# Moving part of the second block's forward Fourier transforms into the first block of a two-layer kernel

## The chip, the cores and the metric

The kernel runs on one core of one Trainium2 chip. The metric is device time in microseconds for one launch, the median of the runs. The core has five engines that run their own instruction streams in order: TensorE (PE in the profile, its weight loads PEld), VectorE (DVE), ScalarE (ACT), GpSimd (POOL) and SyncE (SP), which in this kernel issues nearly all the DMA transfers.

## The reference, cut to what matters

Two layers run one after the other on an input of 4 batches, 128 channels and 128 x 128 positions, all in float32.

```python
# layer 0, per batch, L = 128*128 positions
xm = relu(xf @ mlp_w1.T + b1) @ mlp_w2.T + b2
x_in, z = split(xm @ in_proj_w.T)                 # 256 channels each
u = silu(causal_conv4(x_in) + conv_b)
dt, Bm, Cm = split(u @ x_proj_w.T, [8, 24])
delta = softplus(dt @ dt_proj_w.T + dt_proj_b)
h[t] = h[t-1] * exp(delta[t] * A) + delta[t] * Bm[t] * u[t]      # 256 channels x 16 states
y = (h[t] . Cm[t]) + u * D
out = (y * silu(z)) @ out_proj_w.T
x1 = silu(group_norm(out, 4 groups)) + x

# layer 1, per batch
a = relu(conv1x1(group_norm(cat(x1, x1), 32 groups)) + agg_b)
weights = softmax(mean(a) @ wg_w.T + wg_b)        # 4 per batch
xf = rfft2(x1)                                    # per image, 128 x 65 complex
product = xf * rfft2(irfft2(xf * filt))           # 4 filters
result = irfft2(sum_f weights[f] * product[f]) + 0.5 * x1
```

The kernel uses that the inner inverse and forward transforms cancel, so that the sum over filters is the square of the spectrum times one weighted filter.

## The kernel before, in words

**First block (`block0`).** A batch is cut into 32 chunks of 512 positions, 128 chunks in all. A chunk is 16 slots long. In each slot VectorE runs two scans (`scans`, L411) over 128 partitions, which hold 32 channels with 4 states each; the decay comes from ScalarE (`exps`, L392), the driving term from GpSimd (`dbu`, L362) or, for every fourth one, from a TensorE transpose (`dbu_turn`, L382). The products with C go to VectorE (L413) or GpSimd (L418), and TensorE adds them over states into `y` (L432). The preparation of the next chunk is spread over the slots of the present one by the table that `pre` returns: each entry is a slot, a phase and a function. For example `z_mm` (L222) stands in slot `NP - 3`, which is slot 13, and its eviction `z_act` in slot 15; `cv_mm` (the folded projection and convolution, L233) in slots 0 and 1, `silu_act` in slot 2.

A dictionary `todo` collects all functions by slot and phase, and a loop at the end of `block0` emits them in the order of the phases: turn, sums, pe, exps, late, act, pool, dbu, early, gate, scans, dve, end. That order is written out by hand (`manual_schedule`) and is the order in which each engine executes. Constants are loaded in `first_constants` before the first chunk and in `later_constants` at the end of slot 4 of the first chunk. Matmul results of the preparation share one PSUM pool `psp` of two rotating buffers (tag `pp`).

**The end of layer 0 (`finish`).** The group norm of a batch needs all of its chunks, so it runs during the chunks of the next batch: in chunks 2 to 17 of that batch two pieces of 512 positions are normalised per chunk, and `x1` is written to DRAM; in the chunks after that `x1` is read again for the aggregation (`agg_mm`, L615, `agg_act`, L619). For the last batch this work is done inside the second block.

**Second block (`block1`).** The work is cut into 64 units: a group of 8 channels (`CC`) of one batch. A unit is three steps of 3, 3 and 2 images. Per step: `over_h` (L788) transforms over h on TensorE, ScalarE evicts half of it (L790), `conjugates` (L795) fills the other half by symmetry on VectorE, `over_w` (L802, L803) transforms over w, ScalarE doubles and squares (L805 to L807), `products` (L813 to L820) multiplies by the weighted filter, GpSimd combines real and imaginary parts (`sums`, L827 and L828), `back_h` and `back_w` (L841, L842, L853) transform back, `residual` (L860) adds the input, and the result is stored. The weighted filter of a unit is made by ScalarE (`term`, L761, four per unit) and GpSimd (`mix`, L767, three per unit). The steps of several units overlap: step t emits `over_h(t)`, `over_w(t - 1)`, `products(t - 2)`, `back_h(t - LAG)` and so on, with `LAG` = 7. The images of a unit (`load`, L754) are loaded one unit ahead, the filters of a channel group (`load_filter`, L748) into one of four buffers.

The order of units: the first 13 channel groups for batches 0, 1 and 2 while batch 3 is being finished, then three groups of batch 3 whose filters were kept, then the last 3 groups for all four batches with the remaining units of batch 3 in between.

Of the kernel before, what the change touches and what calls it, by code (L numbers as in the profile page):

```python
# [26 lines left out]
F32 = mybir.dt.float32  # L27
# [6 lines left out]
P = 128  # L34
# [4 lines left out]
CC = 8  # L39
KEEP = 4  # L40
# [5 lines left out]
def kernel(ctx: ExitStack, tc: tile.TileContext, a: dict, out: bass.AP):  # L46
# [32 lines left out]
    def first_constants(s):  # L79

        s.b1 = col("mlp_b1")
        s.w2 = const("w2", [P, NH, C], a["mlp_w2T"].rearrange("(j p) c -> p j c", p=P))
        s.b2 = col("mlp_b2")
        win = s.win = const("win", [P, 2 * DI], a["in_wT"])
        wck = s.wck = const("wck", [P, KC, DI], a["conv_wT"].partition_broadcast(P))
        s.cb = col("conv_b")
        s.wx = const("wx", [P, NH, NX], a["x_wT"].rearrange("(j p) r -> p j r", p=P))
        s.wdt = const("wdt", [R, DI], a["dt_wT"])
        s.bdt = col("dt_b")
        s.ident = const("ident", [P, P], a["c_ident"])  # L90
        alog = const("alog", [P, NH * NG * ND], a["alog_q"])
# [6 lines left out]
        amat = s.amat = cpool.tile([P, NH * NG * ND], F32, tag="amat", name="amat")  # L98
        nc.scalar.activation(amat, alog, AF.Exp)
        nc.vector.tensor_scalar_mul(amat, amat, -1.0)  # L100
        s.diag = cpool.tile([P, NH, P], F32, tag="diag", name="diag")
        for j in range(NH):
            nc.vector.tensor_scalar_mul(s.diag[:, j, :], s.ident, dvec[:, j : j + 1])

    def later_constants(s):
# [7 lines left out]
        s.wagg = const("wagg", [P, 2, C], a["agg_wT"].rearrange("(j p) o -> p j o", p=P))  # L113
# [8 lines left out]
        s.ihc = const("c_ihc", [H, H], a["c_ihc"])  # L122
        s.ihs = const("c_ihs", [H, H], a["c_ihs"])
        s.iw = const("c_iw", [W, W], a["c_iw"])
        s.sign = const("c_sign", [W, H], a["c_sign"])
# [23 lines left out]
    stats, outs = {}, {}  # L149
# [5 lines left out]
def block0(tc, s):  # L155
# [4 lines left out]
    with ExitStack() as ctx:  # L160
# [7 lines left out]
        dbc = pool("dbc", 2, space=DRAM)  # L168
        psp = pool("psp", 2, space=PSUM)
# [13 lines left out]
        def pre(k):  # L183
# [130 lines left out]
            def rep_load(j):  # L314
# [9 lines left out]
                (NP - 3, "pe", z_mm), (NP - 1, "act", z_act), (NP + 2, "act", z_silu), (3, "pe", xd_mm), (4, "act", xd_act), (5, "pe", dt_mm), (5, "pe", xd_turn),  # L324
# [141 lines left out]

        n_chunks = B * NCH
# [20 lines left out]
        for b in range(B - 1):  # L488
            for at, phase, f in finish(s, io, b, NP + 7, norm, agg):
                todo[at + (b + 1) * NCH * NP, phase].append(f)  # L490
        for n in range(n_chunks * NP):
# [182 lines left out]
def block1(tc, s):  # L674
# [10 lines left out]
    with ExitStack() as ctx:  # L685
        def pool(name, bufs, **kw):
            return ctx.enter_context(tc.tile_pool(name=name, bufs=bufs, **kw))

        p2 = pool("f2", 2)
# [7 lines left out]
        fh, fwr, fwi, ihc, ihs, iw = s.fh, s.fwr, s.fwi, s.ihc, s.ihs, s.iw  # L697
        sign = s.sign.rearrange("w (o r k) -> w o r k", o=1, r=2)
# [23 lines left out]
        units = [(c0, b) for c0 in wait for b in range(B - 1)] + [(c0, B - 1) for c0 in kept]  # L722
        for n, c0 in enumerate(rest):
            units += [(c0, b) for b in range(B)]
# [25 lines left out]
        def load(n):  # L750
            if n < N:
                c0, b = units[n]
                u[n].xt = p2.tile([H, CC, W], F32, tag="xt1", name=f"xt1_{n}", bufs=6)
                nc.sync.dma_start(out=u[n].xt, in_=s.x1[b][c0 : c0 + CC].rearrange("c h w -> h c w"))  # L754

# [29 lines left out]
        def over_h(e, n, m, k):  # L785
            e.pa = psa.tile([W, 3, 2, WF], F32, tag="pa", name=f"pa_{n}_{m}")
# [6 lines left out]
        def conjugates(e, n, m, k):  # L793
            o = e.sa[:, 0:k, :, HH:]
# [3 lines left out]
        def over_w(e, n, m, k):  # L798

            e.px = psx.tile([H, 3, 2, WF], F32, tag="px", name=f"px_{n}_{m}")  # L800
            for q in range(k):
                nc.tensor.matmul(images(e.px)[:, q], e.sa[:, q, 0, :], fwr, start=True, stop=False)  # L802
                nc.tensor.matmul(images(e.px)[:, q], e.sa[:, q, 1, :], fwi, start=False, stop=True)  # L803
            e.xs = p2.tile([H, 2, 3, WF], F32, tag="xs", name=f"xs_{n}_{m}")
# [179 lines left out]
```

## Time and profile before

| | |
|---|---|
| median of 3 runs | 7226.67 us (7223.53 to 7229.71) |
| span of the profiled execution, first to last instruction | 7219.4 us |
| median of the runs less that span | 7.3 us |
| first block, to the first instruction of the second | about 6408 us |
| second block | about 811 us |
| DMA traffic | 1246.27 MB, mean 173 GB/s |

The profile is one execution, taken by the hardware profiler; its own time is known as the span in the table. In its slices each digit is the busy share of an engine in tenths. A row of a group gives the line, the engine, the operation, the tiles written and read, their shape and the count, then the time in which the group was busy and the mean duration of one instruction in nanoseconds, and then the idle time of the engine before these instructions with what ended it. A float32 matmul shows as two records. A row of a timeline gives the start, the duration, the engine and the instruction, with the idle time before it in brackets. "SPq" is SyncE issuing a transfer.

### The profile page before, as it was taken

To read this page: it belongs to the slowest core of one execution; us is meant where nothing else is said; L and a number is where in the kernel's file an instruction comes from. 1 tells how busy PE (TensorE), PEld (TensorE's weight loads), DVE (VectorE), ACT (ScalarE), POOL (GpSimd) and SP (SyncE) were. 2 spreads that over 40 slices of the span, in tenths; PEclk is the share of its full clock that TensorE was granted. 3 is DMA by queue.
4 is the path that set the end of the run, shared out by engine and by line. 5 is a ranking of instruction groups with operands and counts; after the bars stand their busy time and mean duration, and the time that the engine had idled before them with its cause. 6 is when DMAs were issued, how large, how long until landed. Compare 5 with 4: busy or idle time off the path is not lost. (4 is left out here: it accounts for less than half of the span.)

```text
span 7219.4 us, 89408 instructions
## 1 busy us (share of the span) xinstructions
PE 5935.8 (82%) x25908; PEld 2629.2 (36%) x25908; DVE 6925.4 (96%) x8040; ACT 6133.6 (85%) x13583; POOL 6890.8 (95%) x3188
## 2 busy tenths in 40 slices
PE   7888888888878788888788788887787888868999
PEld 2333333322222233332222233332232323348999
DVE  7999999999999999999999999999999999978677
ACT  7888888888888888888888888888888888877876
POOL 7999999999999999999999999999999999977787
PEclk8888888888888898998888899998888898989999
DMA  6766676677777776777777777777787777768666
GB/s 151 160 159 160 151 165 159 151 165 172 180 192 178 182 172 161 175 169 170 190 179 192 174 160 176 171 160 187 179 192 181 169 173 169 161 167 240 183 169 164
DMA packets 864127, 1246.27 MB, mean 173 GB/s; under 512 B 78856, under 2 KB 318608, under 8 KB 863632
## 3 DMA queue, kind: packets, MB, share of 16 engines
q1 hardware_dynamic: 863488, 1240.28, 71.8%
q8 instruction: 204, 3.34, 0.2%
q14 instruction: 291, 2.38, 0.1%
q10 hardware_dynamic: 144, 0.26, 0.0%
HBM read 996.97 MB, written 243.27 MB: 172 GB/s over the span
## 5 line engine op out<-in xcount | busy, mean ns | idle before, releaser
L362 POOL TENSOR_TENSOR hb<-rdu,rB 128x1536 f32<-128x1536 f32 (+2 forms) x1536 | 3608.0, 2366 | 35.1 <-DMA rdu<-dd 32.1
L392 ACT ACTIVATE da<-rdelta,amat 128x512 f32<-128x512 f32 x4096 | 2786.1, 698 | 139.3 <-DVE h L411 134.5
L418 POOL TENSOR_TENSOR hb<-h,rC 128x1024 f32<-128x1024 f32 (+1 forms) x1072 | 2436.8, 2275 | 68.4 <-DVE h L411 53.9
L411 DVE TENSOR_TENSOR_SCAN da<-da,st,hb 128x512 f32<-128x512 f32 x1976 | 2417.4, 1265 | 22.1 <-ACT da L392 15.6
L432 PE MATMUL y<-hb,sel 128*32 128x512 f32 x8192 | 1337.9, 730 | 4.7 <-POOL hb L418 4.1
L382 PE MATMUL b<-ident,bt 128*128 128x128 f32 x4096 | 753.9, 307 | 673.5 <-DVE h L411 539.1
L413 DVE TENSOR_TENSOR hb<-da,rC 128x512 f32<-128x512 f32 x2040 | 1294.3, 672 | 3.0
L411 DVE TENSOR_TENSOR_SCAN h<-da,st,b 128x512 f32<-128x512 f32 x992 | 1256.2, 1266 | 1.5 <-PE b L382 1.5
L411 DVE TENSOR_TENSOR_SCAN h<-da,st,hb 128x512 f32<-128x512 f32 x1000 | 1249.9, 1254 | 1.4 <-ACT da L392 1.0
L233 PE MATMUL pp_cv<-xm,wck 128*128 128x512 f32 x2048 | 1061.0, 665 | 1.4 <-ACT xm L216 0.8
L303 ACT ACTIVATE bt<-pt_dut,xdt 128x256 f32<-128x256 f32 x2048 | 836.3, 470 | 186.0 <-PE pt_dut L292 185.8
L382 PEld LDWEIGHTS b<-ident,bt 128*128 128x128 f32 x4096 | 525.5, 154 | 1242.1 <-DVE h L411 902.5
L414 ACT COPY st<-da 128x1 f32<-128x1 f32 x2040 | 271.3, 159 | 495.0 <-DVE hb L413 494.7
L233 PEld LDWEIGHTS pp_cv<-xm,wck 128*128 128x128 f32 x2048 | 417.3, 215 | 706.5 <-issue 460.8
L767 POOL TENSOR_TENSOR wb<-wb,term 128x1040 f32<-128x1040 f32 x192 | 461.1, 2402 | 89.8 <-ACT term L761 78.6
L292 PE MATMUL pt_dut<-ident,du 128*128 128x128 f32 x1024 | 233.7, 339 | 299.9 <-ACT xdt L285 174.0
L428 PE MATMUL y<-u,diag 128*128 128x512 f32 x512 | 300.9, 671 | 149.7 <-DVE zs L442 147.6
L292 PEld LDWEIGHTS pt_dut<-ident,du 128*128 128x128 f32 x1024 | 132.5, 163 | 618.6 <-POOL du L311 492.3
L392 ACT ACT_TABLE_LOAD x262 | 336.1, 1283 | 11.8 <-DMA rdelta<-dd 7.1
L311 POOL TENSOR_TENSOR du<-delta,u 128x512 f32<-128x512 f32 x256 | 319.6, 1271 | 26.7 <-ACT delta L274 26.7
L432 PEld LDWEIGHTS y<-hb,sel 128*32 128x32 f32 x8192 | 173.3, 116 | 371.4 <-issue 278.0
L266 PE MATMUL pp_dt<-xd,wdt 8*128 8x512 f32 x512 | 281.9, 639 | 31.9 <-ACT pp_o L456 23.4
(145 smaller groups left out, 8082.0 us busy)
## 6 DMA issues: line engine op xcount, KB each, us to landing
rdelta<-dd SPq DMA_DIRECT2D x1024, 256.0 KB, 4.7
rdu<-dd SPq DMA_DIRECT2D x1024, 256.0 KB, 7.8
rC<-bc SPq DMA_DIRECT2D x512, 256.0 KB, 7.5
rB<-bc SPq DMA_DIRECT2D x512, 192.0 KB, 4.7
dd<-delta SPq DMA_DIRECT2D x256, 256.0 KB, 7.4
dd<-du SPq DMA_DIRECT2D x256, 256.0 KB, 5.9
ft<-in_filt_w SPq DMA_DIRECT2D x104, 520.0 KB, 6.9
ob<-o SPq DMA_DIRECT2D x128, 256.0 KB, 2.0
```

What stands on the lines that cost most here:

```text
L233: nc.tensor.matmul(ps["cv", j], w, d["xm"][:, t : t + T], start=t == 0, stop=t == KC - 1)
L292: nc.tensor.transpose(ps["dut"][:, 2 * t + j, :], d["du"][:, j, at : at + P], s.ident)
L303: nc.scalar.activation(d["bt"][:, 2 * h + t, :, q, :], src, AF.Copy, scale=d["xdt"][:, 2 * h + t, R + q : R + q + 1])
L311: nc.gpsimd.tensor_tensor(du, d["delta"][:, j, :], d["u"][:, j, :], ALU.mult)
L362: nc.gpsimd.tensor_tensor(hb[:, p : p + n, :], d["du", j][:, m : m + n, :], d["B"][:, p - 1 : p - 1 + n, :], ALU.mult)
L382: nc.tensor.transpose(b[:, t * P : (t + 1) * P], src, s.ident)
L392: nc.scalar.activation(da, d["delta", j][:, m, :], AF.Exp, scale=s.amat[:, c : c + 1])
L411: nc.vector.tensor_tensor_scan(o, das[q], b, init, ALU.mult, ALU.add)
L413: nc.vector.tensor_tensor(hb[:, p + q, :], das[q], d["C"][:, p + q, :], ALU.mult)
L418: nc.gpsimd.tensor_tensor(hb[:, ps, :], h[:, q, :], d["C"][:, ps, :], ALU.mult)
L432: nc.tensor.matmul(y[m * DG : (m + 1) * DG, :], s.sel, d["hb", j, r][:, p, :], start=False, stop=r == NG - 1)
L767: nc.gpsimd.tensor_tensor(wb, wb, u[n].terms[f], ALU.add)
```

## The change

A new list of functions, `spectrum`, is added to the first block. For batch 0 and for the first nine channel groups of batch 1 it loads images from `x1`, transforms them over h and then over w on TensorE, with both halves of the second transform computed into separate halves of the partitions, and stores the result in a DRAM tensor `spec`. A channel group takes three chunks (3, 3 and 2 images). Batch 0 takes chunks 52 to 99 and batch 1 chunks 100 to 126. The units concerned are 25 of 64.

In the second block such a unit loads its spectrum beside its images, and `over_h`, `conjugates` and the matmuls of `over_w` are left out for it; the doubling and the squares read the loaded spectrum. The order of batches within a group becomes 0, 2, 1 (and 0, 2, 1, 3 in the last groups). The projection `z_mm` moves from slot 13 to slot 14. Four constants that only the second block uses are now loaded there, the aggregation weights share a buffer of the normalisation, and a new constant `fwm` is loaded and negated on VectorE.

```diff
+EARLY = 2
...
-        s.wagg = const("wagg", [P, 2, C], a["agg_wT"].rearrange("(j p) o -> p j o", p=P))
+        s.wagg = s.spare.tile([P, 2, C], F32, tag="xr", name="wagg")
+        nc.sync.dma_start(out=s.wagg, in_=a["agg_wT"].rearrange("(j p) o -> p j o", p=P))
...
-        s.ihc = const("c_ihc", [H, H], a["c_ihc"])
-        s.ihs = const("c_ihs", [H, H], a["c_ihs"])
-        s.iw = const("c_iw", [W, W], a["c_iw"])
-        s.sign = const("c_sign", [W, H], a["c_sign"])
+        s.fwm = const("fwm", [W, 2 * WF], a["c_fwi"])
+        nc.vector.tensor_scalar_mul(s.fwm, s.fwm, -1.0)
...
-    stats, outs = {}, {}
+    stats, outs, spectra = {}, {}, set()
+    spec = [dpool.tile([H, C, 2, WF], F32, tag=f"spec_{b}", name=f"spec_{b}") for b in range(EARLY)]
...
-                (NP - 3, "pe", z_mm), (NP - 1, "act", z_act), (NP + 2, "act", z_silu), (3, "pe", xd_mm), (4, "act", xd_act), (5, "pe", dt_mm), (5, "pe", xd_turn),
+                (NP - 2, "pe", z_mm), (NP - 1, "act", z_act), (NP + 2, "act", z_silu), (3, "pe", xd_mm), (4, "act", xd_act), (5, "pe", dt_mm), (5, "pe", xd_turn),
...
+        def spectrum(b, c0, n):
+
+            g = {}
+
+            def load():
+                g["x"] = p1.tile([s.H, 3, s.W], F32, tag="fx", name=f"fx_{b}_{c0}")
+                nc.sync.dma_start(out=g["x"][:, 0:n], in_=s.x1[b][c0 : c0 + n].rearrange("c h w -> h c w"))
+
+            def over_h():
+                g["pa"] = psp.tile([s.W, 3, 2 * s.WF], F32, tag="pp", name=f"pp_fa_{b}_{c0}")
+                for q in range(n):
+                    nc.tensor.matmul(g["pa"][:, q], g["x"][:, q], s.fh, start=True, stop=True)
+
+            def evict():
+                g["sa"] = p1.tile([s.W, 3, 2 * s.WF], F32, tag="fs", name=f"fs_{b}_{c0}")
+                nc.scalar.copy(g["sa"][:, 0:n], g["pa"][:, 0:n])
+
+            def over_w():
+                half = s.H // 2
+                g["px"] = psp.tile([s.H, 3, 2 * s.WF], F32, tag="pp", name=f"pp_fx_{b}_{c0}")
+                for q in range(n):
+                    re, im = g["sa"][:, q, 0 : s.WF], g["sa"][:, q, s.WF :]
+                    for (data, a, b_), start in (((re, s.fwr, s.fwr), True), ((im, s.fwi, s.fwm), False)):
+                        for at, w in ((0, a), (1, b_)):
+                            o = g["px"][at * half : (at + 1) * half, q]
+                            nc.tensor.matmul(o, data[:, at : at + half], w, start=start, stop=not start)
+
+            def store():
+                x = p1.tile([s.H, 3, 2, s.WF], F32, tag="fq", name=f"fq_{b}_{c0}")
+                nc.scalar.copy(x[:, 0:n].rearrange("h c r k -> h c (r k)"), g["px"][:, 0:n])
+                nc.sync.dma_start(out=s.spec[b][:, c0 : c0 + n], in_=x[:, 0:n])
+
+            return [
+                (4, "pe", load), (12, "pe", over_h), (12, "end", evict), (13, "pe", over_w), (13, "end", store),
+            ]
+
         n_chunks = B * NCH
         todo = defaultdict(list)
         for k in range(n_chunks):
...
+        chunk = NCH + NCH // 2 + 4
+        for b in range(EARLY):
+            for c0 in range(0, C, CC):
+                chunk = max(chunk, (b + 1) * NCH + NCH // 2 + 4)
+                if chunk + 3 > n_chunks:
+                    break
+                for at, n in ((0, 3), (3, 3), (6, 2)):
+                    for slot, phase, f in spectrum(b, c0 + at, n):
+                        todo[slot + chunk * NP, phase].append(f)
+                    chunk += 1
+                s.spectra.add((c0, b))
         for n in range(n_chunks * NP):
             if n % 2 == 0:
                 todo[n - 3, "early"].append(partial(exps, n, (0,)))
...
-        fh, fwr, fwi, ihc, ihs, iw = s.fh, s.fwr, s.fwi, s.ihc, s.ihs, s.iw
-        sign = s.sign.rearrange("w (o r k) -> w o r k", o=1, r=2)
+        def const(name, shape):
+            t = late.tile(shape, F32, tag=name, name=name)
+            nc.sync.dma_start(out=t, in_=s.a[name])
+            return t
+
+        fh, fwr, fwi = s.fh, s.fwr, s.fwi
+        with tc.manual_schedule():
+            sign = const("c_sign", [W, H])
+            ihc, ihs, iw = const("c_ihc", [H, H]), const("c_ihs", [H, H]), const("c_iw", [W, W])
+        sign = sign.rearrange("w (o r k) -> w o r k", o=1, r=2)
...
-        units = [(c0, b) for c0 in wait for b in range(B - 1)] + [(c0, B - 1) for c0 in kept]
+        units = [(c0, b) for c0 in wait for b in (0, 2, 1)] + [(c0, B - 1) for c0 in kept]
-            units += [(c0, b) for b in range(B)]
+            units += [(c0, b) for b in (0, 2, 1, 3)]
...
+                u[n].early = units[n] in s.spectra
+                if u[n].early:
+                    u[n].sx = p2.tile([H, CC, 2, WF], F32, tag="sx", name=f"sx_{n}", bufs=2)
+                    nc.sync.dma_start(out=u[n].sx, in_=s.spec[b][:, c0 : c0 + CC])
...
@@ -783,6 +844,8 @@
 
         @block
         def over_h(e, n, m, k):
+            if u[n].early:
+                return
             e.pa = psa.tile([W, 3, 2, WF], F32, tag="pa", name=f"pa_{n}_{m}")
             for q in range(k):
                 nc.tensor.matmul(images(e.pa)[:, q], u[n].xt[:, m + q, :], fh, start=True, stop=True)
...
@@ -791,6 +854,8 @@
 
         @block
         def conjugates(e, n, m, k):
+            if u[n].early:
+                return
             o = e.sa[:, 0:k, :, HH:]
             nc.vector.tensor_tensor(o, e.pa[:, 0:k, :, 1:], sign.to_broadcast([W, k, 2, HH]), ALU.mult)
 
...
@@ -798,10 +863,16 @@
         def over_w(e, n, m, k):
 
             e.px = psx.tile([H, 3, 2, WF], F32, tag="px", name=f"px_{n}_{m}")
+            e.xs = p2.tile([H, 2, 3, WF], F32, tag="xs", name=f"xs_{n}_{m}")
+            if u[n].early:
+                x = e.x = u[n].sx[:, m : m + k]
+                nc.scalar.activation(e.px[:, 0:k, 0], x[:, :, 1], AF.Copy, scale=2.0)
+                nc.scalar.activation(e.xs[:, 0, 0:k], x[:, :, 0], AF.Square)
+                nc.scalar.activation(e.px[:, 0:k, 1], x[:, :, 1], AF.Square)
+                return
             for q in range(k):
                 nc.tensor.matmul(images(e.px)[:, q], e.sa[:, q, 0, :], fwr, start=True, stop=False)
                 nc.tensor.matmul(images(e.px)[:, q], e.sa[:, q, 1, :], fwi, start=False, stop=True)
-            e.xs = p2.tile([H, 2, 3, WF], F32, tag="xs", name=f"xs_{n}_{m}")
             nc.scalar.activation(e.xs[:, 1, 0:k], e.px[:, 0:k, 1], AF.Copy, scale=2.0)
             nc.scalar.activation(e.xs[:, 0, 0:k], e.px[:, 0:k, 0], AF.Square)
             nc.scalar.activation(e.px[:, 0:k, 1], e.px[:, 0:k, 1], AF.Square)
...
-            nc.vector.tensor_tensor(sq[:, 1, 0:k], e.px[:, 0:k, 0], e.xs[:, 1, 0:k], ALU.mult)
+            twice = e.x[:, :, 0] if u[n].early else e.xs[:, 1, 0:k]
+            nc.vector.tensor_tensor(sq[:, 1, 0:k], e.px[:, 0:k, 0], twice, ALU.mult)
```

More of the change, by code (lines that the diff above doesn't have):

```diff
@@ L90, in first_constants @@
         s.ident = const("ident", [P, P], a["c_ident"])
-        alog = const("alog", [P, NH * NG * ND], a["alog_q"])
+        amat = s.amat = const("amat", [P, NH * NG * ND], a["alog_q"])
         dvec = col("D")
@@ L96, in first_constants @@
             nc.vector.tensor_mul(wck[:, t, :], win[:, 0:DI], wck[:, t, :])
-        amat = s.amat = cpool.tile([P, NH * NG * ND], F32, tag="amat", name="amat")
-        nc.scalar.activation(amat, alog, AF.Exp)
+        nc.scalar.activation(amat, amat, AF.Exp)
         nc.vector.tensor_scalar_mul(amat, amat, -1.0)
@@ L168, in block0 @@
         dbc = pool("dbc", 2, space=DRAM)
+        s.spare = p2
         psp = pool("psp", 2, space=PSUM)
@@ L687, in pool @@
             return ctx.enter_context(tc.tile_pool(name=name, bufs=bufs, **kw))
+        late = pool("late", 1)
         p2 = pool("f2", 2)
```

## The prediction

> **What bounds the kernel now.** I read the page first: span and engine totals, then the slices.
>
> ```profile
> span 7219.4 us, 89408 instructions
> PE 5935.8 (82%) x25908; PEld 2629.2 (36%) x25908; DVE 6925.4 (96%) x8040; ACT 6133.6 (85%) x13583; POOL 6890.8 (95%) x3188
> DVE  7999999999999999999999999999999999978677
> POOL 7999999999999999999999999999999999977787
> ```
>
> VectorE and GpSimd are full for 35 of 40 slices, the first block; in the last five, the second block, they are not. So I asked for the busy times by stage. The first two rows are one chunk each (one under the normalisation of the batch before, one under its aggregation), the others are stages of the second block, cut where a unit's last residual ends.
>
> ```profile
> core 0: us, PE busy (x) PEld busy (x) DVE busy (x) ACT busy (x) POOL busy (x), PEclk, DMA share, GB/s
> 3512.60:3562.90 50.30, 39.96 (x154) 14.71 (x153) 50.27 (x54) 43.27 (x95) 50.06 (x24) 0.87 0.76 184
> 4509.50:4558.10 48.60, 41.31 (x160) 15.55 (x159) 48.41 (x51) 42.87 (x97) 47.72 (x22) 0.93 0.73 167
> 6462.00:6658.60 196.60, 170.38 (x1438) 165.44 (x1438) 169.41 (x376) 152.88 (x302) 145.60 (x76) 0.98 0.84 253
> 6658.60:6716.00 57.40, 54.26 (x469) 52.73 (x468) 45.95 (x109) 46.04 (x98) 47.26 (x25) 1.00 0.63 170
> 6716.00:6795.40 79.40, 79.40 (x612) 70.94 (x611) 53.53 (x127) 65.12 (x145) 58.32 (x31) 1.00 0.73 205
> 6795.40:6848.60 53.20, 53.20 (x409) 47.45 (x408) 35.67 (x84) 43.38 (x97) 38.84 (x21) 1.00 0.62 174
> 6848.60:6937.80 89.20, 88.67 (x781) 87.52 (x780) 70.46 (x172) 73.74 (x155) 77.62 (x41) 1.00 0.44 119
> ```
>
> A first-block chunk is VectorE's: 0.03 us idle of 50.30 in the first row, while TensorE and ScalarE have 10 and 7 us free. In the second block TensorE binds from 6716 on (no idle at all to 6848.6), and before that, under the last batch's normalisation, nothing is full on average but the DMA engines are 84% busy.
>
> **The part that shrinks: the second block.** Of 64 units, 25 lose both forward transforms (16 of batch 0, 9 of batch 1). The costs come from the groups of the stage 6716 to 6795:
>
> ```profile
> L767 POOL TENSOR_TENSOR wb<-wb,term 128x1040 f32<-128x1040 f32 x18 | 43.2, 2402 | 11.8 <-ACT term L761 11.0
> L788 PE MATMUL pa<-c_fh,xt 128*128 128x130 f32 x96 | 13.6, 275 | 0.0
> L795 DVE TENSOR_TENSOR sa<-pa,c_sign 128x384 f32<-128x384 f32 (+1 forms) x18 | 9.2, 513 | 24.2 <-ACT sa L790 24.2
> ```
>
> A unit sends TensorE 48 matmuls (8 pa, 16 px, 16 pz, 8 po). In the steady units near 6940 it takes 10.72 us with TensorE never idle, so the 24 forward ones are half: 5.36 us. VectorE loses three conjugate multiplies, 3 x 0.513 = 1.5 us; ScalarE three copies, 3 x 0.43 = 1.3 us (row L790, 432 ns). The three squares and doublings stay, now reading SBUF. GpSimd keeps everything: 3 x 2.402 + 1.30 + 1.29 (sums, L827 and L828) = 9.8 us. So an early unit can fall to about 10 us and no lower, GpSimd being next; an ordinary one stays at 10.72, or 13.29 with three aggregation matmuls in it. The unit order puts an ordinary unit between two early ones in the first nine groups, and one early to two ordinary ones in groups 9 to 12.
>
> By stages: 6716 to 6795.4 is six units of 13.29, four of them early: 4 x 10.1 + 2 x 12.9 = 66, -13 us. 6795.4 to 6848.6, two of four early: 2 x (13.29 - 10.1), plus a little carried into the next, -7. 6848.6 to 6937.8, two of eight: -3.5 (10.9 becomes 9.9, and 0.8 carried each). 6658.6 to 6716, three of five: -5. After 6937.8 only three units are early, and each stands directly before one that waits for its images: TensorE sat 4.2 us at 6988 until "xt<-x" landed, queued behind four filter loads. That wait swallows what the early unit gains; with its spectrum load also in the queue I take +1.
>
> Normalisation, 6462 to 6658.6, fifteen units. They run at 12.67 us with three stalls, none of it from one full engine: the waits name ScalarE, VectorE and TensorE in turn. Without the forward half an early unit should run near 10.8, so two of three give 11.4, and with the stalls about 178, -18 us. **A DMA rule against this.** Three such units (6474.7 to 6512.9) keep the DMA engines 88% busy at 264 GB/s, which at 100% is 300 GB/s: 10.0 MB per three units. Two spectra add 2 x 0.53 MB, so at 300 GB/s the floor is 11.1 / 0.300 = 37 us, 12.3 us a unit and a gain of only 12 us. The Trainium skill, "DMA: Bandwidth & Descriptors", section Specifications, gives some 358 GB/s from HBM to a core: 11.1 / 0.358 = 31 us, 10.3 a unit, no floor at all and -18. These packets are mostly 512 bytes, so I lean to the row; 4 KB runs of a spectrum should be cheaper than that mean, so -16.
>
> **A clock rule against it.** An early unit leaves TensorE idle 4 us. The skill, "TensorE: Matmul & The Clock Gate", part 1, says that an idle window of about 3.4 us halves the clock. This trace agrees (unit at 6981 to 6999: granted clock 0.81 after the 4.2 us gap; one unit takes 17.98 us). But the idle comes in three parts of 1.3 us between back transforms; by the row the clock stays at 1.0 and the sum stands. By the rule, had it come in one piece, each ordinary unit behind an early one would pay up to 1.7 us, half a window, 16 x 1.7 = 27 us, and the gain would be gone.
>
> **What is added, block two's start.** Four constants (sign, ihc, ihs, iw) are now issued by SyncE ahead of the first images. SyncE stood from 6406.4 to 6408.3 waiting for the last "ob<-o" to land; four issues at 0.43 us fit there: nothing, and 1.7 us if they don't. The first spectrum, 0.53 MB at 300 GB/s, goes ahead of the filters for which GpSimd starts: +1.6.
>
> **What is added, the first chunk.** The new tile fwm is negated on VectorE in the list where before only two memsets stood:
>
> ```profile
> 66.85 0.06 DVE L127 MEMSET eps<- 128x1 f32 x1
> 66.89 0.17 DVE L129 MEMSET ones<- 128x128 f32 x1
> 75.88 0.43 SPq L71 DMA_DIRECT2D c_ihc<-in_c_ihc  x1
> ```
>
> VectorE runs in order and reaches the place at 66.85. The load of fwm is the sixteenth constant, in the place of c_ihc, issued at 75.88; c_fwi, the same array, took 2.3 us to land. So VectorE stands still from 66.9 to about 78.3, and behind it wait the scans, then GpSimd's products with C, ScalarE's exponentials (their buffers come free by scans), all of the chunk. 11.4 us, of which 1 to 2 us come back, since the chunk after has that much VectorE idle: +11 (with the multiply). If GpSimd's later DMA wait (4 us idle near 101) absorbs part, +5.
>
> **What is added, 75 chunks.** Chunks 52 to 126 each take a third of a group: one load (0.2 MB) and one store (0.2 MB) on SyncE's queue, six forward and twenty-four half-wide matmul instructions, two ScalarE copies of 128x390. VectorE and GpSimd get nothing. DMA: +0.4 MB on 8.3 to 9.3 MB, 5%, with the engines at 73 to 76%: hidden. SyncE: the store waits for its copy late in slot 13; next in its queue are normalisation loads for five slots later and the second replica load at slot 16. Hidden. ScalarE: 2 x 0.48 = 0.96 of 6 to 7 us free. TensorE: a 130-column instruction goes every 0.11 us (612 in 79.4 us is 0.13 with long ones among them); 6 x 0.12 = 0.7, and 24 x 0.12 = 2.9, or 1.5 if the two halves run side by side as the four quarter-wide y<-hb matmuls do (8 in 1.06 us, against 4 full ones of pp_z in 1.99). 2.2 to 3.6 us, twice that at half clock, into 7 to 11 free. So averages hide it all; the question is the place. Slots 12 to 14:
>
> ```profile
> 3002.18 1.99 PE L222 MATMUL pp_z<-xm,win 128*128 128x512 f32 x4
> 3007.25 0.62 PE L382 MATMUL b<-ident,bt 128*128 128x128 f32 x3 [3.08 <-DVE h L411]
> ...
> 4552.74 1.30 ACT L392 ACTIVATE da<-rdelta,amat 128x512 f32<-128x512 f32 x2
> 4554.60 2.44 DVE L411 TENSOR_TENSOR_SCAN da<-da,st,hb 128x512 f32<-128x512 f32 x2
> ```
>
> TensorE has a hole of 3.08 us there in which the half transform fits, and moving pp_z one slot later costs nothing in it. The exponential that the scan at 4554.60 needs ends about 4553.4: 1.2 us of room. The two copies stand ahead of it and take 0.96, and the second waits for TensorE's half transform, up to some 0.5 us more. So in tight chunks VectorE may lose 0 to 0.4 us; chunk at 3007 has 1.5 us of room and some ScalarE idle, and loses nothing. About half the chunks tight: 75 x 0.5 x 0.2 = +8, bounds 0 and 75 x 0.6 = 45 (at half clock). Not below nothing by more than 5: the filled hole may keep the clock up.
>
> **Sum.** +11 + 8 + 1.6 - 16 - 5 - 13 - 7 - 3.5 + 1 = -23. The profiled span 7219.4 becomes 7196.5; the median of the runs, 7226.67, is 7.3 above that span, so 7203.8.
>
> **Rivals.**
> - Larger gain. The DMA engines give more than 300 GB/s and elasticity between units lets TensorE's spare time reach the ordinary units (-24, -6, -18, -9, -8, -3), first-chunk wait +5, chunks 0, start +1.6: -61, 7165. For it: unit at 6500, 4.13 MB in 12.85 us, 321 GB/s. Against: small buffers (one pa, two px).
> - Nothing measurable. The normalisation stage is held by DMA entirely (0 in place of -16): -7, 7220.
> - Slower: the copies wait on TensorE in nearly every chunk. Priced at 0.75 us of VectorE time per chunk, 75 chunks cost 56 in place of 8: 7252. For it: 0.03 us of VectorE idle means that nothing can be made up; ScalarE's queue is in order. It decides from 0.41 us a chunk (31 / 75). Against: 1.2 to 1.5 us of room before 0.96 us of copies.
>
> **Numbers.** A measurement of this kernel tells some 0.2%, 14.5 us, from no change. Forecast 0.50 (own range 7186 to 7222), larger gain 0.18, nothing 0.18, slower 0.14. Within the forecast's range a sixteenth or so lies inside 0.2%. Faster 0.48 + 0.18 = 0.66, within 0.2% 0.20, slower 0.14. Range 7172 to 7246.
>
> **What would show it.** Right: an early unit near 10 us with GpSimd fullest, ordinary ones unchanged; VectorE idle for some 11 us at 67 in the first chunk; chunk lengths 48.4 to 50.3 as before within 0.3 us; "pp_z" after the new matmuls without a wait that reaches VectorE. Wrong: chunks longer by over half a microsecond, normalisation units still 12.7, TensorE at half clock after early units, or more "xt<-x" waits.

## The result

The changed kernel takes 7174.42 us (median of 4 runs, 7164.74 to 7175.93) against 7225.45 us for the kernel before (4 runs, 7223.53 to 7229.71): a ratio of 0.9926, 95% interval 0.9914 to 0.9939. That is 51 us; the forecast was 23, and 7174 lies nearer to the "larger gain" rival's 7165 than to the forecast's 7203.8. The profiled executions differ by 7219.4 - 7173.6 = 45.8 us, and this is the sum that the terms below must meet. The other 5 us lie in which executions were profiled: the median of the runs is 7.3 us above the profiled span before, and 0.9 us after. Run again beside the last experiments, the changed kernel gave 7173.34 us, ratio 0.9925 (0.9911 to 0.9940), and a span of 7171.8 us.

The page of the kernel after, its first two parts:

```profile
span 7173.6 us, 91384 instructions
PE 5904.2 (82%) x26708; PEld 2626.8 (37%) x26708; DVE 6892.9 (96%) x7966; ACT 6143.9 (86%) x13658; POOL 6892.5 (96%) x3188
DVE  6999999999999999999999999999999999989777
POOL 6999999999999999999999999999999999988887
```

Only the first slice of the first block and the last five slices differ. Busy time by stage, after; the columns are those of the prediction's table, and each row stands for the row at the same place there (chunks 70 and 90, then the second block cut after the same units). "Unit 9" below is the stretch from the end of unit 8's last residual to the end of unit 9's; since steps overlap, the forward transforms that run in it are mostly those of unit 12:

```profile
core 0: us, PE busy (x) PEld busy (x) DVE busy (x) ACT busy (x) POOL busy (x), PEclk, DMA share, GB/s
3522.03:3572.32 50.29, 40.72 (x183) 16.10 (x182) 50.26 (x54) 43.94 (x97) 50.10 (x24) 0.90 0.78 193
4519.86:4568.76 48.90, 41.61 (x176) 15.52 (x175) 48.48 (x51) 43.24 (x99) 48.10 (x23) 0.93 0.71 171
6466.80:6639.10 172.30, 126.01 (x960) 118.28 (x960) 156.18 (x346) 139.52 (x271) 146.90 (x76) 0.95 1.02 317
6639.10:6690.40 51.30, 43.38 (x332) 41.34 (x333) 42.02 (x101) 42.67 (x89) 46.66 (x24) 0.93 0.80 224
6690.40:6756.60 66.20, 62.11 (x445) 52.49 (x444) 48.91 (x117) 60.33 (x135) 58.26 (x31) 1.00 0.94 270
6756.60:6803.20 46.60, 45.62 (x337) 39.24 (x336) 33.08 (x80) 41.30 (x93) 39.06 (x21) 1.00 0.77 226
6803.20:6889.20 86.00, 82.59 (x708) 81.17 (x707) 68.87 (x169) 71.62 (x150) 77.30 (x41) 0.98 0.49 136
6889.20:7169.50 280.30, 251.68 (x2119) 248.46 (x2117) 203.94 (x484) 194.47 (x398) 217.85 (x114) 0.96 0.69 182
```

A chunk with a third of a spectrum in it is as long as before (50.29 against 50.30; 48.90 against 48.60). Over the 75 chunks the mean length differs by 0.01 us, single chunks by up to 1.9 us either way. In the stage under the normalisation, the first row of the second block, TensorE lost 44 us of work and the stage 24 us, with the DMA engines at 1.02 of their time (the profile adds up the times of packets, which can overlap). (The start of a stage is the end of its predecessor's last residual.)

The terms of the prediction's sum, each read from the two traces at the same chunk or unit:

| term | predicted, us | measured, us |
|---|---|---|
| first chunk, fwm | +11 | +10.7 (offset at chunk 52) |
| 75 chunks with a spectrum | +8 | -1.4 (chunk 52 to the block's last eviction) |
| start of the second block | +1.6 | -4.5 (to the end of unit 0) |
| normalisation, 15 units | -16 | -24.3 |
| next four stages | -5, -13, -7, -3.5 | -6.1, -13.2, -6.6, -3.2 |
| tail | +1 | +2.7 |
| sum | -23 | -45.9 |

The second execution of the changed kernel gives +11.3, -1.5, -4.6, -24.8 for the first four.

### The profile page after: what moved, and what is told of

Same layout as the page of the kernel before. It is cut to its first block, busy times and chain, and to the rows that moved or that the text cites. A ratio compares the mean times of both kernels' runs of the same rounds, so it can differ in the third digit from the quotient of the medians.

```text
span 7173.6 us, 91384 instructions
## 1 busy us (share of the span) xinstructions
PE 5904.2 (82%) x26708; PEld 2626.8 (37%) x26708; DVE 6892.9 (96%) x7966; ACT 6143.9 (86%) x13658; POOL 6892.5 (96%) x3188
## 3 DMA queue, kind: packets, MB, share of 16 engines
q8 instruction: 210, 3.44, 0.2%
## 4 chain that ended last, share of the span: by engine, by line
DVE 41%; ACT 29%; issue 11%; PE 10%; DMA 5%; POOL 3%; SPq 1%; DVEq 0%; ACTq 0%; POOLq 0%
DVE da L412 20%; DVE h L412 12%; ACT da L393 12%; DVE hb L414 5%; ACT L393 3%; DMA rdelta<-dd 2%; ACT L275 2%; ACT delta L275 2%; ACT bt L304 2%; POOL hb L363 2%; DVE zs L443 1%; PE y L433 1%; POOL hb L419 1%; ACT L242 1%; DMA xt<-x 1%
## 5 line engine op out<-in xcount | busy, mean ns | idle before, releaser
L433 PE MATMUL y<-hb,sel 128*32 128x512 f32 x8192 | 1313.4, 717 | 2.9 <-POOL hb L419 2.7
L234 PE MATMUL pp_cv<-xm,wck 128*128 128x512 f32 x2048 | 1014.3, 640 | 1.6 <-ACT xm L217 0.8
L234 PEld LDWEIGHTS pp_cv<-xm,wck 128*128 128x128 f32 x2048 | 395.9, 204 | 651.0 <-issue 422.1
L312 POOL TENSOR_TENSOR du<-delta,u 128x512 f32<-128x512 f32 x256 | 318.8, 1267 | 25.8 <-ACT delta L275 25.8
L223 PE MATMUL pp_z<-xm,win 128*128 128x512 f32 x512 | 274.5, 634 | 51.8 <-ACT fq L497 46.2
```

The source lines that it names most:

```text
L234: nc.tensor.matmul(ps["cv", j], w, d["xm"][:, t : t + T], start=t == 0, stop=t == KC - 1)
L312: nc.gpsimd.tensor_tensor(du, d["delta"][:, j, :], d["u"][:, j, :], ALU.mult)
L433: nc.tensor.matmul(y[m * DG : (m + 1) * DG, :], s.sel, d["hb", j, r][:, p, :], start=False, stop=r == NG - 1)
```

## The experiments

Ratios are to the kernel before, run on the same chip beside each. Times of stages come from each kernel's one profiled execution.

### The wait for fwm, and what it uncovered

The wait itself is where it was expected; VectorE's timeline of the kernel after in chunk 0 (start, duration, instruction, idle time before):

```profile
65.16 1.22 DVE L412 TENSOR_TENSOR_SCAN h<-da,hb 128x512 f32<-128x512 f32 x1 [0.25 <-ACT da L393]
77.38 0.23 DVE L124 TENSOR_SCALAR fwm<-fwm 128x130 f32<-128x130 f32 x1 [11.00 <-DMA fwm<-in_c_fwi]
```

First the negation alone was moved:

```diff
-        nc.vector.tensor_scalar_mul(s.fwm, s.fwm, -1.0)      # later_constants, chunk 0
+        todo[3 * NP + 4, "end"].append(lambda: s.nc.vector.tensor_scalar_mul(s.fwm, s.fwm, -1.0))
```

> The changed kernel with the negation of fwm moved from chunk 0 to chunk 3, so that VectorE never stands for the load. My theory: the wait in chunk 0 is carried undiminished to the end of the first block, so chunk 1 starts 9 to 11 us sooner than in the changed kernel (about 106 us in place of 116.6) and the whole takes 7163 to 7166 us against 7174. Rival: later chunks or the normalisation stage have room that swallowed the wait, and the whole stays within 7171 to 7177 us.

Measured: 7169.87 us, ratio 0.9929 (0.9914 to 0.9944), between the ranges of both theories and not told from the changed kernel's 0.9926. Chunk 1 starts at 110.6 us, 5.9 sooner than in the changed kernel's trace, and chunk 4 is 0.6 us later again. Neither theory had the reason. The 11 us wait is gone, but two multiplications on VectorE got longer. Its timeline in this kernel, with weff0's product (weff in the rows) in chunk 0 and the negation in chunk 3:

```profile
78.08 10.37 DVE L132 TENSOR_SCALAR weff<-wagg,gn_gamma 128x128 f32<-128x128 f32 x1
...
223.00 6.54 DVE L511 TENSOR_SCALAR fwm<-fwm 128x130 f32<-128x130 f32 x1
229.46 2.46 DVE L411 TENSOR_TENSOR_SCAN da<-da,st,hb 128x512 f32<-128x512 f32 x2
```

and GpSimd's at the second place:

```profile
220.15 3.61 POOL L362 TENSOR_TENSOR hb<-rdu,rB 128x1024 f32<-128x1024 f32 x2
223.69 2.39 POOL L418 TENSOR_TENSOR hb<-h,rC 128x1024 f32<-128x1024 f32 x1
226.01 3.44 POOL L362 TENSOR_TENSOR hb<-rdu,rB 128x1536 f32<-128x1536 f32 x1
235.53 2.35 POOL L418 TENSOR_TENSOR hb<-h,rC 128x1024 f32<-128x1024 f32 x1 [6.08 <-DVE h L411]
```

A negation that takes 0.23 us while GpSimd stands took 6.54 us, and ends at 229.54, just after GpSimd's last instruction in a row (226.01 + 3.44 = 229.45). Scans and tensor_tensor instructions beside the same GpSimd work keep their usual times (every tensor_tensor of L413 in the kernel before takes 0.66 to 0.69 us). They differ from the multiplications that wait in more than the operation: in this kernel one of their two inputs lies in PSUM. So both parts went to ScalarE:

```diff
-        nc.vector.tensor_scalar_mul(s.fwm, s.fwm, -1.0)
+        todo[3 * NP + 4, "end"].append(lambda: s.nc.scalar.mul(s.fwm, s.fwm, -1.0))
...
-        nc.vector.tensor_scalar_mul(weff0, s.wagg[:, 0, :], s.gam[:, 0:1])
-        nc.vector.scalar_tensor_tensor(weff0, s.wagg[:, 1, :], s.gam[:, 1:2], weff0, ALU.mult, ALU.add)
+        nc.scalar.activation(weff0, s.wagg[:, 0, :], AF.Identity, scale=s.gam[:, 0:1])
+        nc.scalar.activation(pb0[:, P : 2 * P], s.wagg[:, 1, :], AF.Identity, scale=s.gam[:, 1:2])
...
+        nc.vector.tensor_add(weff0, weff0, pb0[:, P : 2 * P])
```

> The changed kernel with the negation of fwm done by ScalarE in chunk 3, and the two products of weff0 in chunk 0 done by ScalarE too, with one tensor_add left to VectorE. In the run that moved the negation on VectorE it took 6.54 us in place of 0.23, and weff0's first product 10.37 us in place of 2.79: both stood until GpSimd had no instruction running. My theory now: VectorE's tensor_scalar waits for GpSimd, so this version, which has none left there, starts chunk 1 at 99 to 101 us (104.1 before, 116.6 changed), and the whole is 13 to 17 us shorter than the changed kernel, 7157 to 7162 us. Rival: the 11 us of chunk 0 are a wait for something else that comes back in another place; chunk 1 starts later than 106 us and the whole stays above 7167 us.

Measured: 7156.66 us, ratio 0.9905 (0.9890 to 0.9920). Chunk 1 starts at 103.1 us, 13.4 sooner than in the changed kernel; 4.2 us of new waiting, for ScalarE, kept it from the 99 to 101 expected. From chunk 52 on the first block stays 13.7 to 17 us ahead of the changed kernel. So a wait of VectorE in chunk 0 is carried to the end of the block in full.

### Are the spectra free in the first block, and is the gain theirs?

```diff
-                u[n].early = units[n] in s.spectra
+                u[n].early = False
```

> The changed kernel whose first block makes and stores all spectra, while the second block ignores them and does every forward transform itself. My theory: the first block ends about 9 us later than before, as in the changed kernel (all of it from the wait in chunk 0), and the second block takes what it took before or 1 to 3 us more (constants loaded at its start), so 7233 to 7240 us against 7225 before. Rival: part of the 55 us that the second block gained comes from the other order of batches and from the constants, and not from the spectra; then the second block is shorter than before here too, and the whole is 7205 to 7228 us.

Measured: 7235.07 us, ratio 1.0018 (1.0009 to 1.0027): the whole is as my theory had it, the parts not quite. The first block ends 8.3 us later than before, and from chunk 52 on loses nothing (it is 10.1 us behind there). The second block takes 8.8 us more than before, not 1 to 3: its start 2.6, and the normalisation stage 6.1:

```profile
6473.00:6675.70 202.70, 173.43 (x1438) 168.99 (x1439) 169.97 (x375) 152.92 (x302) 145.53 (x76) 0.97 0.81 245
```

To see whether the order of batches makes those 6 us, the kernel before got that order alone:

```diff
-        units = [(c0, b) for c0 in wait for b in range(B - 1)] + ...
+        units = [(c0, b) for c0 in wait for b in (0, 2, 1)] + ...
-            units += [(c0, b) for b in range(B)]
+            units += [(c0, b) for b in (0, 2, 1, 3)]
```

> The kernel before with one edit: the batches of a group come in the order 0, 2, 1. In the run that ignored the spectra the normalisation stage took 202.7 us in place of 196.6 before. My theory: the order alone costs these 6 us, so this stage takes 201 to 204 us and the whole 5 to 8 us more than before. Rival: the 6 us come from the constants loaded at the second block's start and the changed places in memory; then the order makes no difference beyond 2 us.

Measured: 7222.66 us, ratio 0.9998 (0.9989 to 1.0007); the stage takes 196.4 us (6466.8 to 6663.2). The order does nothing, and the theory falls. Looked at unit by unit, the two kernels differ in how many units are long and at a lower clock. Units 8 and 9 of the kernel before; unit 9 is one of those whose images are loaded behind the filters of the next group:

```profile
6551.40:6564.10 12.70, 11.29 (x99) 10.91 (x98) 11.27 (x26) 10.25 (x22) 9.73 (x6) 1.00 0.99 259
6564.10:6579.40 15.30, 12.77 (x102) 12.61 (x102) 11.47 (x26) 10.11 (x21) 9.66 (x6) 0.89 0.81 270
```

Such a filter-loading unit takes 12.7 to 13.7 us at clock 1.00, or 15.1 to 15.8 at 0.89. Before, two of the five are long (units 9 and 12), and the same two with the other order; with spectra ignored, four (3, 9, 12 and 15); units 3 and 15 are 2.2 and 2.8 us longer than before, 5.0 of the 6.1. In each long unit TensorE waits once for 2.5 to 3.0 us, in all but one of these eight for images; in the others, no wait is longer than 2.3 us. TensorE's waits for images in the whole stage, before and with the spectra ignored:

```profile
PE pa L788 <- DMA xt<-x: 8.2, 4, 2.7
PE pa L851 <- DMA xt<-x: 13.7, 5, 3.0
```

These 5.5 us more are nearly the 6.1. That the waits make the long units is shown by a run that comes up again under "The tail": the kernel before with images loaded ahead of filters. In it no wait for images is left in the stage, all fifteen units take 12.7 us at clock 1.00, and the stage is 6.5 us shorter than before:

```profile
6467.90:6658.00 190.10, 168.28 (x1435) 162.52 (x1435) 168.66 (x375) 153.21 (x302) 145.73 (x76) 1.00 0.86 261
```

Why the images come later with the spectra ignored than before stays open. In the changed kernel the filter-loading units are early ones; they show a clock of 0.84 or 0.85 too, but TensorE is busy for only 7.4 to 7.8 of some 11 us in them, and they are shorter than their neighbours.

What a spectrum chunk has left was measured by adding ScalarE work to it:

```diff
-                nc.scalar.copy(x[:, 0:n]..., g["px"][:, 0:n])
+                for _ in range(3):
+                    nc.scalar.copy(x[:, 0:n]..., g["px"][:, 0:n])
```

> The changed kernel with the copy of each spectrum (pp_fx to fq) done three times in a row, 0.98 us more of ScalarE's time in each of the 75 chunks. My theory: a spectrum chunk is free because its ScalarE work fits into the time that is left before the exps of slot 15 are due (0.5 to 1.7 us in the changed kernel's chunks); 0.98 us more does not fit in the tight chunks, and the stretch from chunk 52 to the end of the first block gets 5 to 40 us longer. Rival: ScalarE's queue has room enough elsewhere, and the stretch stays within 3 us.

Measured: 7202.75 us, ratio 0.9969 (0.9957 to 0.9980), as expected. The stretch from chunk 52 to the end of the block is 34.4 us longer than before, 35.9 longer than in the changed kernel: 0.48 us a chunk for 0.91 us of copies (0.98 in a chunk of three images, less in one of two). VectorE's waits in the stretch (us in total, times, longest), in the kernel after:

```profile
engine line waited for: us in total, times, longest us
DVE da L412 <- ACT da L393: 11.4, 6, 2.9
```

with the copies tripled:

```profile
DVE da L412 <- ACT da L393: 32.3, 35, 3.9
```

and before, without spectra:

```profile
DVE da L411 <- ACT da L392: 13.9, 15, 2.0
```

So a chunk has room for the one copy and some 0.4 us more, on average, and then the room is gone. The spectra themselves fitted.

### What limits the normalisation stage?

Two runs changed only the transfers of early units. One loads the first unit's spectra alone (of 25 loads it leaves out 24, not the 34 of its expectation):

```diff
-                if u[n].early:
+                if u[n].early and n:
+                    u[n].sx = u[0].sx
+                elif u[n].early:
```

> The changed kernel, which loads the spectra of the first unit only and uses them for all early units (so it leaves out 34 loads of 0.53 MB and its result is not the reference's). My theory: the normalisation stage is now set by the DMA engines at 317 GB/s; without 9 or 10 loads of 0.53 MB it shrinks by up to 16 us, until VectorE's 156 us of work is next, so the stage takes 157 to 163 us in place of 172.3 and the whole 7159 to 7166 us. Rival: the stage is set by the order of the engines' work and not by transfers, and stays at 170 to 173 us, the whole at 7171 to 7176 us.

```profile
6468.50:6634.90 166.40, 124.72 (x960) 116.73 (x960) 155.39 (x346) 140.04 (x271) 146.27 (x76) 0.96 0.98 297
```

The other copies each spectrum once more, from DRAM to DRAM:

```diff
                     nc.sync.dma_start(out=u[n].sx, in_=s.spec[b][:, c0 : c0 + CC])
+                    nc.sync.dma_start(out=s.spare_spec[:, c0 : c0 + CC], in_=s.spec[b][:, c0 : c0 + CC])
```

> The changed kernel with one more transfer in each early unit: the spectra that it loads are also copied within the chip's memory, 0.53 MB read and 0.53 MB written, with no engine's work added. My theory: the DMA engines are full in the normalisation stage, so each of its early units gets 1.5 to 3 us longer: the stage 187 to 203 us in place of 172.3, the whole 7189 to 7210 us, and later stages, where DMA has room, hardly move. Rival: no change beyond 3 us.

```profile
6465.65:6647.30 181.65, 131.83 (x960) 124.90 (x960) 156.35 (x346) 139.65 (x271) 146.25 (x76) 0.91 1.03 329
```

Measured: 7162.96 us, ratio 0.9920 (0.9905 to 0.9935), and 7189.52 us, ratio 0.9956 (0.9939 to 0.9973). Without the loads the stage is 5.9 us shorter, with the copies 9.4 us longer. Both directions are as my theory had them and both sizes in the stage are too small: it asked for 9 to 15 less and at least 15 more. The whole times lie in its ranges, since the stages behind shrank and grew by some 4 us too. Transfers matter here, but below their price: taking 5.2 MB away (317 GB/s x 172.3 us less 297 x 166.4) returned 5.9 us, where they take 16 us at 317 GB/s. The rate is no constant: by the rows' shares the spectra took 12.7 us of the DMA engines' time (1.02 x 172.3 less 0.98 x 166.4), some 410 GB/s, and the rest of the traffic moves at 303 (297 / 0.98). And VectorE's 155 us of work are 93% of the 166.4. Neither is a bound by itself.

Then the spectra of batch 1 were left out:

```diff
-EARLY = 2
+EARLY = 1
```

> The changed kernel with spectra of batch 0 alone; the nine units of batch 1 in groups 0 to 8 do their forward transforms themselves again. My theory: 27 chunks with a spectrum less change nothing in the first block (within 2 us); in the second, where both kinds of unit count, about half of the gain behind the start goes: the stage from unit 0 to unit 15 takes 180 to 188 us (172.3 with both, 196.6 with none), the stretch from unit 15 to unit 30 takes 172 to 182 us (164.2 with both, 190.0 with none), and the whole is 7191 to 7203 us. Rival: in the normalisation stage the transfers alone set the time, so that the five units of batch 1 there are worth nothing; then it stays at 172 to 176 us.

```profile
6466.40:6644.60 178.20, 145.11 (x1200) 138.29 (x1200) 162.07 (x362) 147.10 (x287) 145.44 (x76) 0.99 0.96 294
```

Measured: 7184.35 us, ratio 0.9941 (0.9926 to 0.9956), under the range of my theory; the stage lies between the two theories' ranges. Of the stage's 24.3 us, batch 0's units bring 18.4 and batch 1's 5.9; of the 25.8 us between the ends of units 15 and 30, 20.6 and 5.2. With five units of each batch in the first and five and four in the second, an early unit of batch 0 is worth about three times one of batch 1 that is added to it. The row of units shows why in part: between two ordinary ones, an early unit also shortens its neighbour (11.2 us in place of 12.7), since steps of several units overlap; and the early unit of batch 0 is the one that loads filters, where the long units were. All units of this run but one have clock 1.00 in this stage.

### The tail

In the kernel after TensorE waits 23.6 us in the tail for images. The view of waits there, after:

```profile
PE pa L851 <- DMA xt<-x: 23.6, 6, 5.3
```

```diff
+                    load(n + 1)
                     for ft in loads[n]:
                         load_filter(ft)
-                    load(n + 1)
```

> The changed kernel with one edit in the second block: at the start of a unit the next unit's images are loaded ahead of the filters, not behind them. My theory: units 40, 43, 47, 50, 54 and 57, which take 12.7 to 18.8 us in place of 10.7, stand only because their images queue behind eight filter loads; they fall to about 10.8 us each and the whole is 20 to 27 us shorter than the changed kernel. Rival: the filters are needed as early as the images, so the wait moves from the images to them and the whole stays within 5 us.

Measured: 7139.65 us, ratio 0.9882 (0.9868 to 0.9897). Against the changed kernel's 0.9926 that is 32 us, more than expected; by the traces the tail is 33.4 us shorter. The wait for images is gone, and so are the lower clocks that came behind it:

```profile
6885.50:7132.40 246.90, 240.83 (x2119) 238.03 (x2117) 201.19 (x484) 192.91 (x398) 218.04 (x114) 1.00 0.77 207
```

The same edit on the kernel before:

> The kernel before, with the one edit that images are loaded ahead of filters in the second block. With it on the changed kernel, the tail from unit 38 to unit 63 fell from 280.2 to 246.9 us; before, this tail takes 277.6 us. My theory: the waits for images in the tail are as large before as after, so it falls to 246 to 252 us here too and the whole is 26 to 34 us shorter than before, 7190 to 7198 us; the three early units of the tail are then worth at most 3 us. Rival: the changed order of batches makes these waits, the kernel before has few of them, and the edit gives it less than 15 us.

```profile
6936.50:7191.30 254.80, 253.27 (x2262) 252.69 (x2261) 206.50 (x492) 197.74 (x407) 218.19 (x114) 1.00 0.74 197
```

Measured: 7198.72 us, ratio 0.9960 (0.9945 to 0.9975), just above the expected range, and a tail of 254.8 us in place of 277.6, 22.8 less where 26 to 32 was expected. The rival is refuted, but my bound on the early units was wrong: in tails without waits they are worth 254.8 - 246.9 = 7.9 us, three units at 2.6 each. In the changed kernel that gain was turned into longer waits for images (13.9 us before, 23.6 after), and the tail got 2.7 us longer. With the images first in both kernels, the change is worth 0.9960 - 0.9882 = 0.0078 of the time, some 56 us, so its gain does not hang on these waits. In the normalisation stage the edit does nothing for the changed kernel (172.3 us without it):

```profile
6467.10:6639.15 172.05, 126.29 (x960) 118.62 (x960) 156.09 (x346) 139.64 (x271) 146.41 (x76) 0.95 1.01 316
```

### All together

```diff
-                chunk = max(chunk, (b + 1) * NCH + NCH // 2 + 4)
-                if chunk + 3 > n_chunks:
+                chunk = max(chunk, NCH + NCH // 2 + 4 if b == 0 else 2 * NCH + NCH // 2 + 4)
+                if chunk + 3 > n_chunks or c0 >= 13 * CC:
```

with the ScalarE edit and the order of loads above:

> Three edits together on the changed kernel: VectorE's negation of fwm and products of weff0 go to ScalarE (7156.7 us alone, ratio 0.9905), images are loaded ahead of filters in the second block (7139.7 us alone, 0.9882), and the spectra are made for the first 13 groups alone, batch 0 in chunks 52 to 90 and batch 1 from chunk 91 for 12 groups, none for the last three groups. If the gains add up: 0.9926 less 0.0021 less 0.0044 is 0.9861, 7125 us, and three more early units of batch 1 in groups 9 to 11, in place of the three of batch 0 in the last groups, give 0 to 6 us more: 7118 to 7126 us. Rival: the parts share one slack and do not add up, above 7133 us.

> The changed kernel once more, unedited, for a comparison on the same chip as these three: 7168 to 7176 us. Theories do not differ on it.

Measured: 7129.08 us, ratio 0.9865 (0.9848 to 0.9881), 44 us under the changed kernel's 7173.34 on the same chip, and the shortest time here. It lies above my theory's range and under the rival's: the two edits alone would add up to 0.9861, 7125 us, so they nearly do, and the choice of groups adds nothing. By the traces it gains, against the changed kernel, 5.0 us from unit 19 to unit 30 and 2.2 from there to unit 38, and its tail has the 254.8 us of a tail without early units, 7.9 more than with them.

## Why the prediction was wrong

The direction and the mechanism in the second block were right, the size was not: half of the gain was missing from the sum.

- **The first chunk, +11:** right, measured +10.7. The idle 11.0 us lies where the prediction put it. That GpSimd's later idle time would absorb part did not happen: it stood too, behind the scans. That the sum meets to 0.3 us is luck: weff0's first product takes from 1.14 to 10.37 us in the three traces with the chunk 0 of the kernel before, and against the one with the other order of batches the offset at chunk 52 is only 6.9 us.
- **75 chunks, +8:** mis-sized; measured -1.4, and -1.8 with the spectra made but not used; the other traces with these 75 chunks unedited lie between -1.1 and -4.7, so they cost nothing. The step that failed is "about half the chunks tight: 75 x 0.5 x 0.2". The room was real (1.2 us) and so were the copies (0.96 us), but 0.96 fits into 1.2. The half microsecond more, in which ScalarE's second copy waits for TensorE's half transform, did not come: in none of the 75 chunks did ScalarE stand idle before that copy. In the timeline of chunk 70 after, the 24 half-wide matmuls take from 3564.27 to 3565.81, 1.5 us, the lower of the two prices given, and pp_z follows them with 0.27 us of waiting (0.6 us a chunk over all 75), which does not lengthen the chunk:

```profile
3564.27 0.44 PE L493 MATMUL pp_fx<-c_fwr,fs 128*64 128x130 f32 x4 [0.17 <-ACT fs L483]
...
3565.54 0.27 PE L493 MATMUL pp_fx<-fwm,fs 128*64 128x130 f32 x1
3565.75 1.13 PE L223 MATMUL pp_z<-xm,win 128*128 128x512 f32 x2
3567.15 1.13 PE L223 MATMUL pp_z<-xm,win 128*128 128x512 f32 x2 [0.27 <-ACT fq L497]
```

  The tripled copies show where the rival "slower" would begin: 0.91 us more in each chunk, on average, costs 36 us.
- **Start of the second block, +1.6:** the sign was wrong. It counted the constants and the first spectrum; with the spectra ignored, the start costs 2.6 us. Left out was the saving: the forward transforms of units 0 to 3 run before the end of unit 0, and three of these four units (0, 2 and 3) are early. That is worth the difference, 2.6 + 4.5 = 7.1 us.
- **Normalisation, -16:** mis-sized; measured -24.3. Two steps failed. The first is the floor of 300 GB/s, which made -16 of -18: the engines gave 317 GB/s over the stage. The page "DMA: Bandwidth & Descriptors" of the Trainium skill, section Specifications, states some 358 GB/s; the estimate from it, -18 without a floor, was nearer than the row's -12, and units 9 and 10 of the changed kernel come near that rate (355 and 349 GB/s between 6558.7 and 6581.5), and unit 7 passes it (369 GB/s from 6535.0 to 6547.0). The second is that the sum kept the stage's stalls. It read that the waits name ScalarE, VectorE and TensorE in turn; TensorE's 8.2 us of waits for images were not counted. Without them the kernel before takes 190.1 us (images ahead of filters), and the changed kernel with the same edit 172.1, so the work saved is 18.0 us, the prediction's own figure. The rest, some 6.5 us, are the stalls: in the changed kernel the units behind the filter loads are early, do no forward transform, and TensorE does not wait for images in them. The sign "ordinary ones unchanged" failed as well: the ordinary units of this stage take 11.4 to 12.0 us in place of 12.7.
- **The clock rule:** the clock was wrong, the time right. The granted clock did fall, to 0.83 to 0.85, in seven of the first nineteen units (3, 6, 9, 12, 15, 16 and 18), where the prediction had it stay at 1.0. TensorE's longest wait in the normalisation stage is 2.3 us, so here the clock fell without the idle window that the prediction's rule asks for. Six of the seven are early units, in which TensorE has room, and none of the six is longer than its neighbours. The 27 us that were weighed did not come.
- **The four stages after it:** -29.1 for -28.5. Here one engine, TensorE, was the bound before, and counting its instructions was enough.
- **Tail, +1:** measured +2.7, by the mechanism named.
- **Span to median, +7.3:** the last step added the 7.3 us by which the median stood above the span before; after, it is 0.9.

Of the 23 us of span that the sum missed, then, 9.4 are the chunks, 6.1 the start, 8.3 the normalisation stage; the rest nearly cancels. The "larger gain" rival had this stage (-24) and the chunks (0) right, and most of the stages behind it and the first chunk too favourable.

## What to carry to other kernels

Before an instruction is put into a full engine's list, look at what it waits for: here one 0.23 us negation made VectorE stand for 11 us, while work on the emptier engines in 75 chunks cost nothing until the gap before the next due exponential was used up. Where one engine is full, count its instructions; where none is, a byte rate read from another mix is not a floor, and a stall that is kept in the sum needs its cause. In a queue that is served in order, what is needed first goes first: one line moved was worth 32 us where the whole change gave 51.

## What the hardware showed that was not expected

**VectorE's tensor_scalar can wait for GpSimd through several of its instructions.** weff0's first product, 128x128 float32, took 1.14, 2.79, 6.84, 10.37 and 10.37 us in five kernels (before, after, before with loads swapped, e_fwm, before with the other order), with the same operands. In e_fwm it lasted through the rest of the GpSimd instruction that was running and four more, until GpSimd had no work; in the kernel after, it got through at GpSimd's first change of instruction. The Trainium skill, "SBUF — State Buffer", section "Summary: rules for kernel authors", says that the second to issue is blocked until the first one finishes, and in section "Who interferes with whom" it counts tensor_scalar among the instructions that can take the ports that VectorE and GpSimd share. The waits agree; that one can last over several instructions of the other engine is what these runs add. What decides when it gets through is open. It also means that the start of chunk 1 differs by 5 us between kernels whose chunk 0 is the same (104.1 and 109.2 us, before and before with the other order), so a few microseconds of a first chunk are not to be explained by an edit elsewhere.
